# A gated recurrent layer on one core: GpSimd's addition for an output goes behind its work on 1-z, and VectorE's addition of two x sums goes to the middle of a half step

## The chip, the core and the metric

The kernel runs on one core of one Trainium2 chip. The engines in this text are TensorE (PE, with its weight loads PEld), VectorE (DVE), ScalarE (ACT), GpSimd (POOL) and the queue that issues transfers (SP). The metric is device time in microseconds (us). Before the change it is 1883.74 us, the median of three runs (1882.47 to 1884.24).

## The reference

All arrays are float32. x is 64 x 128 x 512 (batch, time, feature). Two layers follow one another, and each adds its input to its result. Layer 0 is a gated scan that isn't touched here. Layer 1 is a recurrence over 128 time steps with a state h of 64 x 512:

```
xz, xr, xh = seq @ W_z, seq @ W_r, seq @ W
def step(h, xs):
    z  = sigmoid(xzt + h @ U_z + vz)
    r  = sigmoid(xrt + h @ U_r + vr)
    hh = tanh(xht + r * h @ U + vh)
    h_new = (1.0 - z) * h + z * hh
    return (h_new, h_new)
x = x + layer1(x)
```

So each output row is the new h plus that time step's x. vz, vr and vh come from a conditioning vector and are the same for all time steps.

## The kernel before, in words

**Two streams.** The 64 batches are cut into two streams of 32 (`SB`), and their time steps alternate: while one stream waits for its gates, TensorE works for the other. One time step of one stream is called a half step in this text, and the function `halves` (a generator) writes it down in two parts. All instructions are pinned, so each engine runs its instructions in the order in which the program names them; nothing is reordered later.

**One half step.** Part one: TensorE multiplies the old state hT with the weights of r and z (the groups `g<-w_s,h`, L464); ScalarE takes the sigmoid of r (L918); VectorE forms r*h and transposes it, in two halves (L922, L923, L922, L923); ScalarE takes the sigmoid of z (L927); GpSimd forms 1-z (L933) and (1-z)*h (L934). Part two: TensorE multiplies the transposed r*h with the candidate's weights (the groups `g<-w_s,fi`, L464, "the candidate group" below); ScalarE takes the tanh (L957); VectorE forms the new h (L969, L970) and transposes it to hT (L974). Then GpSimd adds x to hT (L985, into the tile hh), and in the next half step, which is the other stream's, VectorE transposes that sum into the output tile (L994, the function `output`, kept in the list `deferred` until then).

**The x products.** The products of x with W_z, W_r and W don't depend on the state. They are computed ahead of the recurrence, for windows of eight time steps, with a fast matrix multiplication in two nested levels (seven products for eight, twice). Its products are TensorE groups at L602 (`r`, `r12a`, `r12b`, `shared`), and `place` puts up to three of them into each half step, to fill TensorE while the gates are worked out. What the scheme costs elsewhere: GpSimd makes sums and differences of x (L810, `take_sums`, into `held`); VectorE reads the products out of PSUM, with an addition to an accumulator in SBUF (L704) or with an addition of a common part (L699), both in `read`; VectorE adds two accumulators, both in SBUF, in `add_c` (L719); GpSimd does the same for another pair in `add` (L724). The finished sums are stored to DRAM (`shares`) and loaded again as a stream's start value for its gates (`load_share`, L865; `put_share`, L871).

**The order around the change.** The mid of a half step, between the two parts, is written like this:

```
add(1)
take_sums(2 if busy else 3)
place(targets()[0], busy)
...
read(reads[0] and max(reads[0], len(to_read) - 2))
while deferred:
    deferred.pop(0)()
```

At the end of part two stand L985, `deferred.append(output)`, then `add_c()` and `read(reads[1])`. `reads` is (4, 1) in the first stretch and (4, 0) later, so mostly up to four reads stand in the mid. `add_c` takes one entry from the list `to_add_c`, if there is one; the reading of the sixth of the seven outer products (`n == 5`) calls it by itself for a block that still waits (`while n == 5 and (m, j) in waiting_c`). `waiting`, `to_add` and `add` are the same for GpSimd. From time step 121 on (`APART`) another form of the half step runs, without L985.

Of the kernel before, what the change touches and what calls it, by code (L numbers as in the profile page):

```python
# [12 lines left out]
ALU = mybir.AluOpType  # L13
# [6 lines left out]
def kernel(  # L20
# [38 lines left out]
    nc = tc.nc  # L59
# [11 lines left out]
    SB = B // 2  # L71
# [7 lines left out]
    def pin(instruction):  # L79
        return tc.keep_in_program_order(instruction)  # L80
# [199 lines left out]
    def chunk_products(g, c, between=None):  # L280

        f, i = fs[c % 2], is_[c % 2]
        fb, ib = by_batch(f), by_batch(i)
        p = gate(g, c, 0)
        pin(nc.scalar.activation(fb, p, AF.Sigmoid, bias=biasT[:, 0, c : c + 1]))
        if g == 0 and c == 0:
            w0_transposed(0, 2)
        elif g == 0 and c + 1 < K:
            w0_transposed(c + 1, 0)
        if between:  # L290
            between()
        p = gate(g, c, 1)
        pin(nc.scalar.activation(ib, p, AF.Sigmoid, bias=biasT[:, 0, K + c : K + c + 1]))
        if g == 0 and c == 0:
            transposed(condT, cond_sb, n=B)
            w0_transposed(1, 0)
        elif g == 0 and c + 1 < K:
            w0_transposed(c + 1, 1)
        if g + 1 < NG:
            for u, m in ((), ((0, 0), (0, 1)), ((1, 0),), ((1, 1),))[c]:  # L300
                x_joined(g + 1, u, m)
        p = gate(g, c, 2)
        if g == 0 and c + 1 < K:
            for n in range(1 if c == 0 else 2, 3):
                w0_transposed(c + 1, n)
        return p
# [135 lines left out]
    def conditioning():  # L442

        vs = []
        for s in range(2):
            p = psum.tile([P, 3, P], F32, tag="tp", name=f"pv{s}")
            matmuls(p, lambda k: condT[:, k, s * SB : (s + 1) * SB], [cw[:, k] for k in range(K)])
            whole = const.tile([P, 3, P], F32, name=f"whole_v{s}")
            pin(nc.vector.tensor_tensor(whole, p, bias1, ALU.add))
            vs.append(whole)  # L450
        return vs
# [106 lines left out]
    def x_of(st, t):  # L558

        return x4[t // TH][:, :, t % TH, st.batches]  # L560
# [4 lines left out]
    class Outer:  # L565
# [121 lines left out]
        def read(self, block, common):  # L687


            (m, j), n, r = block, self.n, self.bank(block)  # L690

            while n in (0, 5) and (m, j) in waiting:
                add(1)
            while n == 5 and (m, j) in waiting_c:
                add_c()
            if j == 1 and not common:
                if not hasattr(self, "common"):
                    shared_to_copy[0]()
                pin(nc.vector.tensor_tensor(r, r, self.common, ALU.add))  # L699
                return  # L700
            u, s5, c = (acc[:, i, m, j] for i in range(3))
            v1, v21 = v_x[:, j], v_x[:, 2 + j]
            dst, other = ((u, v1), (c, u), (u, u), (s5, v21), (c, s5), (u, u), (c, u))[n]
            pin(nc.vector.tensor_tensor(dst, r, other, ALU.add))  # L704
            unread.discard(r.name)
            if n == 1:
                self.store(c, 0, m, j)
            elif n == 4:
                waiting_c.add((m, j))
                to_add_c.append(lambda: self.add_c(c, u, m, j))  # L710
            elif n == 5:
                waiting.add((m, j))
                to_add.append(lambda: self.add(s5, u, m, j))
            elif n == 6:
                self.store(c, 1, m, j)

        def add_c(self, c, u, m, j):
            waiting_c.remove((m, j))
            pin(nc.vector.tensor_tensor(c, c, u, ALU.add))  # L719
            self.store(c, 0, m, 2 + j)  # L720

        def add(self, s5, u, m, j):
            waiting.remove((m, j))
            pin(nc.gpsimd.tensor_tensor(s5, s5, u, ALU.add))  # L724
            self.store(s5, 1, m, 2 + j)
# [13 lines left out]
    to_copy, shared_to_copy = [], []  # L739
    to_read, unread = [], set()  # L740
# [12 lines left out]
    sums_to_take, taken = [], set()  # L753
# [12 lines left out]
    def sum_tasks(group):  # L766
# [24 lines left out]
        def halves(d):  # L791
            *ts, op = d
            return [(*[t[:, k] for t in ts], op) for k in range(HC)]

        outer = [
            [(base - 1, ("s", group, i, k), d_) for k, d_ in enumerate(halves(d))]
            for i, d in enumerate(wsums(x_[0][0], x_[0][1], x_[1][0], x_[1][1], s_))
        ]
# [6 lines left out]
    def take_sums(n):  # L805
        for m in range(n):
            if not sums_to_take or sums_to_take[0][0] > state["begun"]:
                return m
            _, name, a = sums_to_take.pop(0)
            pin(nc.gpsimd.tensor_tensor(*a))  # L810
            taken.add(name)
        return n

    ahead = []
# [21 lines left out]
    class Stream:  # L836
# [56 lines left out]
        def halves(self, t, filler=None, between=None, targets=lambda: (0, 0), busy=False, reads=(4, 0)):  # L893
# [40 lines left out]
                    pin(nc.gpsimd.tensor_tensor(r, r, h_, ALU.mult))  # L934
            while shared_to_copy:
                shared_to_copy[0]()
            add(1)
            take_sums(2 if busy else 3)
            place(targets()[0], busy)
            if filler:  # L940
                filler()
            read(reads[0] and max(reads[0], len(to_read) - 2))
            while deferred:
                deferred.pop(0)()
# [4 lines left out]
            h, hT, hh = (tile_[:, n] for n in range(3))  # L949
# [31 lines left out]
            if apart:  # L981
                deferred.append(output)
                return
            pin(
                nc.gpsimd.tensor_tensor(  # L985
                    hh.rearrange("p (k b) -> p k b", b=SB),
                    hT.rearrange("p (k b) -> p k b", b=SB),
                    x_of(self, t),
                    ALU.add,
                )  # L990
            )

            def output():
                pin(nc.vector.transpose(o, hh))  # L994
                self.store(t)

            deferred.append(output)
            if APART <= t + AHEAD < S:

                pin(nc.gpsimd.tensor_copy(ident.rearrange("p (k b) -> p k b", b=SB), x_of(self, t + AHEAD)))  # L1000
                deferred.append(lambda: pin(nc.vector.transpose(self.output(t + AHEAD), ident)))
            add_c()
            read(reads[1])
            if t + 2 < S and not direct(self, t + 2) and all((t + 2, q) in stored for q in range(Q)):
                self.load_share(t + 2)
# [29 lines left out]
    APART, AHEAD = 121, 10  # L1035
    last_outputs = []
    deferred = []
    pending = []

    shares_d = [dram.tile([TW * B, Q, 3 * P], F32, name=f"shares{n}") for n in range(4)]  # L1040

    for g in range(NG):
        for c in range(K):
# [7 lines left out]
            if (g, c) == (1, 1):  # L1051
                vs = []
                p = chunk_products(g, c, between=lambda: vs.extend(conditioning()))
            else:
                p = chunk_products(g, c)
# [154 lines left out]
    for n in range(2):  # L1210
        t = work.tile([P, 5, 3, P], F32, tag="xt", bufs=2, name=f"w_inner{n}")
# [94 lines left out]
        n += len(steps)  # L1306
    while deferred:
        deferred.pop(0)()
    assert not ahead and not to_read and not to_copy and not shared_to_copy and not sums_to_take


# [32 lines left out]
```

## Time and profile before

| | |
|---|---|
| median of the three runs | 1883.74 us |
| the profiled execution, its own time | 1881.64 us |
| its span, from the first to the last instruction | 1879.9 us |
| TensorE busy | 1864.0 us, 99% of the span |
| VectorE busy | 1504.4 us, 80% |
| GpSimd busy | 864.1 us, 46% |
| granted TensorE clock | 1.00 |
| layer 1 in the trace | from about 684 us to the end |
| VectorE's additions L719 | 60, mean 556 ns |
| GpSimd's additions L985 | 242, mean 501 ns |

The profile is of one execution. "Busy" is the time in which an engine has an instruction; the number behind an `x` counts instructions (a float32 matmul leaves two records). A timeline row gives the start in us from the span's start, the duration in us, engine, line, operation, the tiles written and read, and, in brackets, the idle time before it and what ended it. Releasers are inferred. Engines that aren't the bottleneck may idle at no cost.

### The profile page before, as it was taken

The numbers are of one execution on the slowest core, as the hardware profiler recorded it, in microseconds if no ns is written. First come the engines' busy times: TensorE is split into PE (matmuls) and PEld (weight loads), VectorE is DVE, ScalarE is ACT, GpSimd is POOL, SyncE is SP. The second block draws the span as 40 slices with busy tenths as digits, with TensorE's granted clock in tenths as the row PEclk, the third lists the DMA queues.
The fourth block names the chain that finished last, engine by engine and source line by source line (L and its number), as shares of the span: only waits on it lengthen the run. The fifth ranks groups of instructions, "written<-read, shape, count | busy, mean of one in ns | idle before, by whom it ended". The sixth has DMA issues, their size and how long they took to land.

```text
span 1879.9 us, 62310 instructions
## 1 busy us (share of the span) xinstructions
PE 1864.0 (99%) x24793; PEld 1061.1 (56%) x24793; DVE 1504.4 (80%) x3438; ACT 722.3 (38%) x1888; POOL 864.1 (46%) x1544
## 2 busy tenths in 40 slices
PE   9999999999999999999999999999999999999998
PEld 5444444444444445666666666666666666666667
DVE  5899999999999977577777777777777777777786
ACT  3232223222232232344444444444444444444444
POOL 1233232333323244446556566566565565565650
PEclk9999999999999999999999999999999999999999
DMA  7765433433343240334334344344343343443343
GB/s 176 182 124 117 84 69 74 88 81 80 73 80 60 49 86 29 96 94 141 104 105 131 108 116 130 100 129 121 101 140 108 99 139 103 115 130 96 111 110 79
DMA packets 366754, 195.38 MB, mean 104 GB/s; under 512 B 225332, under 2 KB 352064, under 8 KB 366464
## 3 DMA queue, kind: packets, MB, share of 16 engines
q1 hardware_dynamic: 366280, 191.33, 41.0%
q8 instruction: 195, 3.19, 0.7%
q14 instruction: 95, 0.78, 0.2%
q10 hardware_dynamic: 184, 0.07, 0.0%
HBM read 78.63 MB, written 81.13 MB: 85 GB/s over the span
## 4 chain that ended last, share of the span: by engine, by line
PE 97%; DVE 1%; issue 0%; DMA 0%; ACT 0%; SPq 0%; DVEq 0%; ACTq 0%
PE g L464 36%; PE p L232 35%; PE r L602 14%; PE r12a L602 4%; PE shared L602 4%; PE r12b L602 4%; PE gz L464 1%; PE tp L190 0%; PE pv L464 0%; DMA x<-in_x_dram 0%; DVE W L704 0%; DMA out_dram<-o_last 0%; DVE fi L923 0%; DVE fi L922 0%; DVE r L339 0%
## 5 line engine op out<-in xcount | busy, mean ns | idle before, releaser
L232 PE MATMUL p<-xT,W 128*128 128x512 f32 (+1 forms) x1560 | 661.9, 586 | 0.1
L232 PEld LDWEIGHTS p<-xT,W 128*128 128x128 f32 x1560 | 293.4, 190 | 361.6 <-issue 359.4
L464 PE MATMUL g<-w_s,h 128*32 128x256 f32 (+1 forms) x8128 | 481.3, 373 | 2.6 <-issue 1.4
L464 PEld LDWEIGHTS g<-w_s,h 128*32 128x32 f32 x8128 | 304.1, 110 | 177.0 <-issue 81.8
L464 PEld LDWEIGHTS g<-w_s,fi 128*32 128x32 f32 x8128 | 222.9, 109 | 116.1 <-issue 57.9
L464 PE MATMUL g<-w_s,fi 128*32 128x128 f32 x8128 | 276.0, 273 | 5.4 <-DVE fi L922 3.9
L922 DVE TENSOR_TENSOR fi<-fi,h 128x64 f32<-128x64 f32 (+1 forms) x494 | 112.5, 228 | 172.3 <-ACT fi L918 171.2
L985 POOL TENSOR_TENSOR h<-h,x 128x128 f32<-128x128 f32 x242 | 121.3, 501 | 234.1 <-DVE h L974 207.8
L314 POOL COPY first<-condT 128x4 f32<-128x4 f32 x64 | 12.4, 194 | 461.7 <-DVE h L386 431.9
L918 ACT ACTIVATE fi<-g 128x128 f32<-128x128 f32 x254 | 70.6, 278 | 324.2 <-PE g L464 305.1
L933 POOL TENSOR_SCALAR fi<-fi 128x128 f32<-128x128 f32 x240 | 71.9, 300 | 239.4 <-DVE fi L922 231.1
L704 DVE TENSOR_TENSOR W<-r,W 128x384 f32<-128x384 f32 x315 | 169.3, 539 | 7.5
L310 ACT ACTIVATE fi<-fi 128x512 f32<-128x512 f32 x64 | 40.3, 630 | 340.4 <-DVE fi L351 340.4
L957 ACT ACTIVATE h<-g 128x128 f32<-128x128 f32 x256 | 71.2, 278 | 241.8 <-PE g L464 241.8
L923 DVE STREAM_TRANSPOSE fi<-fi 128x64 f32<-128x64 f32 (+1 forms) x494 | 122.2, 247 | 22.8 <-PE r12a L602 0.5
L969 DVE TENSOR_TENSOR h<-h,fi 128x128 f32<-128x128 f32 (+1 forms) x264 | 93.8, 355 | 53.9 <-ACT h L957 53.1
L253 POOL TENSOR_TENSOR x<-xT,h 128x512 f32<-128x512 f32 x63 | 122.6, 1946 | 4.9
L934 POOL TENSOR_TENSOR fi<-fi,h 128x128 f32<-128x128 f32 x240 | 110.2, 459 | 20.0
L970 DVE TENSOR_TENSOR h<-h,fi 128x128 f32<-128x128 f32 (+1 forms) x264 | 97.6, 370 | 27.2 <-POOL held L810 0.9
L602 PE MATMUL r<-w_inner,held 128*32 128x384 f32 x1080 | 114.8, 486 | 0.0
L810 POOL TENSOR_TENSOR held<-held 128x128 f32<-128x128 f32 x240 | 112.9, 485 | 3.1
L339 DVE RECIPROCAL r<-r 128x256 f32<-128x256 f32 x60 | 104.4, 1740 | 0.0
(153 smaller groups left out, 2727.7 us busy)
## 6 DMA issues: line engine op xcount, KB each, us to landing
shares<-W SPq DMA_DIRECT2D x240, 192.0 KB, 2.0
xz<-shares SPq DMA_DIRECT2D x480, 48.0 KB, 1.9
whole_v<-shares SPq DMA_DIRECT2D x480, 48.0 KB, 1.9
x2d<-x SPq DMA_DIRECT2D x63, 256.0 KB, 4.5
words<-held SPq DMA_DIRECT2D x240, 64.0 KB, 2.1
out_dram<-o SPq DMA_DIRECT2D x240, 64.0 KB, 1.8
xw_None<-x2d SPq DMA_DIRECT2D x56, 256.0 KB, 3.3
w_rows<-in_L_cond_W_f_dram SPq DMA_DIRECT2D x4, 256.0 KB, 5.8
```

Source lines behind the costliest of these rows:

```text
L232: nc.tensor.matmul(p[:, tokens], lhsT=W0[:, c, n, k, :], rhs=xT[g][:, k, tokens], start=(k == 0), stop=(k == K - 1),)
L253: nc.gpsimd.tensor_tensor(x2.rearrange("p (t b) -> p t b", b=GB)[:, ts], xT[g][:, c, :].rearrange(f"{layout(g)} -> p t b", b=GB)[:, ts], b ...
L339: pin(nc.vector.reciprocal(r, r))
L464: nc.tensor.matmul(p[q * SB : (q + 1) * SB], lhsT=lhsT(k), rhs=part(wk, q), start=(start and k == 0), stop=(stop and k == len(w) - 1), ski ...
L602: nc.tensor.matmul(self.bank(bank)[q * SB : (q + 1) * SB], lhsT=a[:, q * SB : (q + 1) * SB], rhs=w_, start=start, stop=True, skip_group_ch ...
L704: pin(nc.vector.tensor_tensor(dst, r, other, ALU.add))
L810: pin(nc.gpsimd.tensor_tensor(*a))
L922: pin(nc.vector.tensor_tensor(rh[:, e], r[:, e], h_[:, e], ALU.mult))
L923: pin(nc.vector.transpose(rhT[:, e], rh[:, e]))
L934: pin(nc.gpsimd.tensor_tensor(r, r, h_, ALU.mult))
L970: pin(nc.vector.tensor_tensor(h[:, e], hh[:, e], r[:, e], ALU.add))
L985: nc.gpsimd.tensor_tensor(hh.rearrange("p (k b) -> p k b", b=SB), hT.rearrange("p (k b) -> p k b", b=SB), x_of(self, t), ALU.add,)
```

## The change

Two things move in `halves`; no instruction is added or taken out.

- L985 is put off. Instead of writing it down at the end of its half step, the code keeps it in a new list `unsummed` and writes it down in the next half step, behind L933 and L934 and ahead of `add(1)` and `take_sums`. It appends `output` to `deferred` only then, and `deferred` is still worked off in that same half step.
- `add_c()` goes from the end of part two to the mid of the half step, ahead of `read`, and runs there only if fewer than four reads are due.

```
             while shared_to_copy:
                 shared_to_copy[0]()
+            while unsummed:
+                unsummed.pop(0)()
             add(1)
             take_sums(2 if busy else 3)
             place(targets()[0], busy)
             if filler:
                 filler()
+            if len(to_read) < 4:
+                add_c()
             read(reads[0] and max(reads[0], len(to_read) - 2))
...
-            pin(
-                nc.gpsimd.tensor_tensor(
-                    hh.rearrange("p (k b) -> p k b", b=SB),
-                    hT.rearrange("p (k b) -> p k b", b=SB),
-                    x_of(self, t),
-                    ALU.add,
-                )
-            )
...
-            deferred.append(output)
+            def summed():
+                pin(
+                    nc.gpsimd.tensor_tensor(
+                        hh.rearrange("p (k b) -> p k b", b=SB),
+                        hT.rearrange("p (k b) -> p k b", b=SB),
+                        x_of(self, t),
+                        ALU.add,
+                    )
+                )
+                deferred.append(output)
+
+            unsummed.append(summed)
...
-            add_c()
             read(reads[1])
...
+    unsummed = []
```

More of the change, by code (lines that the diff above doesn't have):

```diff
@@ L1308 @@
         deferred.pop(0)()
-    assert not ahead and not to_read and not to_copy and not shared_to_copy and not sums_to_take
+    assert not ahead and not to_read and not to_copy and not shared_to_copy and not sums_to_take and not unsummed
 _INS = [
```

## The prediction

> **What bounds the kernel now.** I read the page's busy times first, then its chain of work that ended last.
>
> ```profile
> PE 1864.0 (99%) x24793; PEld 1061.1 (56%) x24793; DVE 1504.4 (80%) x3438; ACT 722.3 (38%) x1888; POOL 864.1 (46%) x1544
> ...
> PE 97%; DVE 1%; issue 0%; DMA 0%; ACT 0%; SPq 0%; DVEq 0%; ACTq 0%
> ```
>
> TensorE is the bound, and the change takes no work from it. So it can only shorten or lengthen waits of TensorE, and these must be found although TensorE counts as busy. In the timeline, the candidate groups (`g<-w_s,fi`) start at 1292.99 and 1297.52: an undisturbed half step takes 4.53 us (5.18 where it holds one more x product of 0.65). I took the distances of all these starts between 720 and 1797 us; what exceeds 4.53 or 5.18 is a stall. The sum is only about 7.5 us, in pieces of 0.02 to 0.5. Next I looked at what lies ahead of such a stall, on all engines.
>
> ```profile
> 1064.73 0.52 DVE L719 TENSOR_TENSOR W<-W 128x384 f32<-128x384 f32 x1
> ...
> 1064.95 0.62 POOL L985 TENSOR_TENSOR h<-h,x 128x128 f32<-128x128 f32 x1 [2.31 <-DVE h L974]
> ...
> 1065.17 0.48 DVE L922 TENSOR_TENSOR fi<-fi,h 128x64 f32<-128x64 f32 x1
> ...
> 1065.68 0.24 DVE L923 STREAM_TRANSPOSE fi<-fi 128x64 f32<-128x64 f32 x1
> ...
> 1066.08 1.08 PE L464 MATMUL g<-w_s,fi 128*32 128x128 f32 x32
> ```
>
> L922 takes 0.23 us undisturbed (0.18 behind another instruction) and 0.48 here. It ends at 1065.65, 0.08 after L985 (1065.57); L985 itself took 0.62 instead of 0.46, as it began during L719. So an addition of VectorE with two inputs in SBUF (L719, L922, L969, L970) and one of GpSimd exclude each other. The transposes and the readers of PSUM (L704, L699) keep their durations beside GpSimd. The transposed r*h releases the candidate group, and that group began 0.21 late. Both halves of the change touch this place.
>
> **Part one: L985 moves behind L933 and L934.** Its 242 executions stay. In half steps with few GpSimd sums L985 now runs alone between L974 and L922; later it runs from about 0.9 to 1.35 us after the candidate group's start, when VectorE reads PSUM. I counted 23 half steps from 853 to 1797 us whose L922 is stretched by L985 and whose sums (L810) are long over; their stalls add up to 2.4 us. Some of these have three sums, which now end 0.4 later and delay L970: 0.2 off. Gain 2.2. Between 1797 and 1836 four such stalls (0.40, 0.20, 0.06, 0.04) give 0.5.
>
> Where L724 and three sums follow, nothing is won: GpSimd runs without a pause to about 3.4 to 4.0 us after the group's start, L985 last. Put first, it pushes L724 and L810 back by its spacing of 0.42, so that the last L810 meets L922 instead. I replayed three kinds of such half steps by the rows of their own instructions (1302.09, 936.60, 867.43): L922 ends within 0.04 of where it did. I take 0; bounds -1.0 and +2.0 over some 40 half steps.
>
> One early stall is large: the candidate group at 714.40 is 2.75 late. There L985 holds back four sums of 128x256 until 709.43, where they alternate with L1278 and three L515, which take about 1.0 each instead of 0.55. After the change these sums no longer wait for L974 and can start about 1.6 earlier, beside PSUM reads. I take 1.0; bounds 0.3 and 1.8.
>
> What waits for L985: L994, next half step. The slack between them was 0.67 to several us; L985 now ends about 1.4 after the group's start, so L994 waits only with one or two reads ahead of it, and delays L969 by up to 0.25. That is covered by VectorE's idle time ahead of L922 (171.2 us in 210 waits). Behind L985 on GpSimd stand L724 and the sums; TensorE starts a product 2.57 us or more after its sum in 95 of 100 cases.
>
> **Part two: L719.** In the order of the built program 46 of the 60 stand behind L974 before and none after. The condition on the reads due holds them back in half steps with four reads, and they pile up. In the listing a half step never had more than one L719 (after 800 us); now eight have three and four have two, always ahead of or between three or four reads. This is such a half step before:
>
> ```profile
> 1292.92 0.24 DVE L923 STREAM_TRANSPOSE fi<-fi 128x64 f32<-128x64 f32 x1
> 1293.26 0.56 DVE L704 TENSOR_TENSOR W<-r,W 128x384 f32<-128x384 f32 x1
> 1293.73 0.56 DVE L699 TENSOR_TENSOR r<-r,x 128x384 f32<-128x384 f32 x1
> 1294.32 0.56 DVE L704 TENSOR_TENSOR W<-r,W 128x384 f32<-128x384 f32 x1
> 1294.79 0.55 DVE L719 TENSOR_TENSOR W<-W 128x384 f32<-128x384 f32 x1
> 1295.26 0.56 DVE L699 TENSOR_TENSOR r12a<-r12a,x 128x384 f32<-128x384 f32 x1
> ...
> 1296.63 0.31 DVE L974 STREAM_TRANSPOSE h<-h 128x128 f32<-128x128 f32 x1
> 1296.87 0.18 DVE L922 TENSOR_TENSOR fi<-fi,h 128x64 f32<-128x64 f32 x1
> ```
>
> VectorE has no idle time left: L922 comes right behind L974, and the next candidate group still starts on time, with 0.05 to spare. The half step gets two more L719, one ahead of the first L704 and one between it and L699. By the spacing of starts (0.44 to 0.48 for each, and 0.16 won since the first need not wait for PSUM) L922 comes 0.74 later. That is TensorE's wait without any exclusion: **0.7**. With it more: rows where L719 meets GpSimd follow.
>
> ```profile
> 779.81 0.72 POOL L933 TENSOR_SCALAR fi<-fi 128x128 f32<-128x128 f32 x1 [5.26 <-DVE fi L922]
> 779.85 0.52 DVE L719 TENSOR_TENSOR W<-W 128x384 f32<-128x384 f32 x1
> ...
> 1589.37 0.46 POOL L934 TENSOR_TENSOR fi<-fi,h 128x128 f32<-128x128 f32 x1
> 1589.47 0.77 DVE L719 TENSOR_TENSOR W<-W 128x384 f32<-128x384 f32 x1
> 1589.78 1.33 POOL L724 TENSOR_TENSOR W<-W 128x384 f32<-128x384 f32 x1
> ```
>
> The first L719 comes right behind L923, as in the first two rows, and delays L933, L934 and L985; the second then meets L934 or L985, the third L724 (+0.2 to +0.4 each by these rows). L922 comes 1.02 later (1.14 if L933 goes first).
>
> - Five half steps of this kind (three L719, four reads), at 1219, 1293, 1367, 1441 and 1515: 4 x 1.0, and 0.3 for the one at 1441, which has an x product more. 4.3 (without exclusion 2.9, at most 4.9).
> - Three at 923, 997 and 1071 (three L719, three reads, one L719 before): 0.9 each less the 0.1 stalled now. 2.4 (0.9 to 2.5).
> - At 1145 a product of TensorE waits for a read (L704 ends 1146.40, L602 starts 1146.45); one L719 is now ahead: 0.4.
> - Three at 1589, 1662 and 1736 (two L719 for one): 0.35 each, 1.05 (0.7 to 1.8).
>
> Sum **8.2**, bounds 4.9 and 9.6. TensorE can't make a wait good: no other work of its order is ready. Transfers: one more start value is loaded at the head of a half step (12 for 11 before); no ScalarE copy L871 waits for a load in the waits view. Cost 0.
>
> The Trainium skill (SBUF — State Buffer, "Who interferes with whom") says that a VectorE instruction with two SBUF inputs and a GpSimd one that reads SBUF exclude each other for the whole instruction, whoever starts first. By that rule a blocked L719 would add its whole 0.52 after the other's end; the row at 1589.47 shows 0.41 (1590.24 less 1589.83). With 0.52 two blocked L719 in each of eleven of these half steps would make the sum 2 us larger. The row decides.
>
> **Sum.** 8.2 - 2.2 - 0.5 - 1.0 = +4.5 us. The profiled execution goes from 1881.64 to 1886.1. Its time is 2.1 below the median, so for the median I say 1883.74 + 4.5 = **1888.2**.
>
> **Rivals.**
> 1. *The additions meet GpSimd less than counted* (order of starts falls well, early gain 1.8). Losses 4.9, gains up to 5.5: -0.6 to +2.5, about 1885. For it: an L719 that starts first isn't slowed. Against: GpSimd is busy at these places without a pause.
> 2. *The late sums now block L922.* In half steps with L724 and three sums L922 waits for an L810 of up to 0.78 instead of an L985 of 0.46: 0.2 more in some 25 half steps, +5, with the sum above +9.5, about 1893. Against: my replays; for: the last L810 is often the longer instruction.
> 3. *Faster: all exclusions vanish.* If the gaps that L985 leaves let the sums end before L922 everywhere, the 7.5 us of stalls, 0.7 at the end and 1.8 early all go: -10.0, and with losses of 4.9 the time is 1878.6. It decides from the point where the twelve crowded half steps cost less than what is won. Against: GpSimd's amount of work is the same, and in 40 half steps it has no gap.
>
> **How the numbers follow.** Forecast (+2.5 to +7) 0.52, rival 1 0.27, rival 2 0.16, rival 3 0.05. The range joins the bounds: losses 4.9 less gains 5.5 gives 1883; losses 9.6, gains 2.2 and +2.0 in the half steps with many sums give 1893. A measurement of this kernel can tell about 0.2% (3.8 us) from no change: slower by more is 0.4 of the forecast's 0.52 and all of rival 2, 0.56; faster by more 0.04; within 0.40.
>
> **What would show it.** In the profile after: L922's stretched executions in half steps without late sums are gone; the half steps named above take 5.2 to 5.6 us from one candidate group to the next, with L974 and L922 late behind three L719; the stall at 714 shrinks. I am wrong if those half steps keep 4.53, or if L922 waits for L810 in many others.

## The result, and the profile after

The changed kernel takes 1889.68 us (median of 6 runs, 1889.42 to 1890.39); the kernel before, on the same chip, 1882.97 (6 runs, 1881.90 to 1884.24). The ratio is 1.0036, with a 95% interval from 1.0026 to 1.0047: 6.7 us slower. The profiled executions have spans of 1888.1 and 1879.9 us, 8.2 apart, at granted clocks of 1.00; the before profile was of one of its quicker executions.

In the code behind the change L985 is L996, and its transpose L994 is L991; L957, L969, L970, L974 are L961, L973, L974, L978. The lines up to L934 keep their numbers. The page after, its busy line and the shares of the chain of work that ended last:

```profile
PE 1865.7 (99%) x24793; PEld 1071.1 (57%) x24793; DVE 1526.7 (81%) x3438; ACT 722.8 (38%) x1888; POOL 858.0 (45%) x1544
...
PE 88%; DVE 6%; POOL 2%; issue 1%; ACT 1%; DMA 0%; SPq 0%; DVEq 0%; POOLq 0%; ACTq 0%
```

TensorE has the same instructions and is busy 1.7 us longer; the rest of the 8.2 are pauses. The chain now runs over VectorE and GpSimd for 8% of the span (before, 1%). The groups of instructions by line, busy time and mean, then idle time before them and its cause:

```profile
L464 PE MATMUL g<-w_s,fi 128*32 128x128 f32 x8128 | 276.1, 273 | 10.6 <-DVE fi L922 9.8
...
L922 DVE TENSOR_TENSOR fi<-fi,h 128x64 f32<-128x64 f32 (+1 forms) x494 | 106.9, 216 | 161.0 <-ACT fi L918 159.8
...
L991 DVE STREAM_TRANSPOSE o<-h 128x128 f32<-128x128 f32 x240 | 73.1, 305 | 52.4 <-POOL h L996 48.1
...
L996 POOL TENSOR_TENSOR h<-h,x 128x128 f32<-128x128 f32 x242 | 113.7, 470 | 3.1 <-DVE h L978 3.1
```

L922 and L996 got shorter (means 228 and 501 ns before): they meet less, as part one should bring. L991 waits 48.1 us for L996, where its wait for GpSimd was 0.6. Most of that stands in place of idle time that was there: VectorE's waits ahead of L922 (for L918) and of L973 (for L961) went from 171.2 and 53.1 to 159.8 and 17.8 us. The candidate group waits 9.8 us for L922, and here the time went. This is the crowded half step whose before-form the prediction shows at 1293, one window later (timeline of after):

```profile
1370.46 0.25 DVE L923 STREAM_TRANSPOSE fi<-fi 128x64 f32<-128x64 f32 x1
...
1370.48 1.08 PE L464 MATMUL g<-w_s,fi 128*32 128x128 f32 x32
1370.59 0.72 POOL L933 TENSOR_SCALAR fi<-fi 128x128 f32<-128x128 f32 x1 [1.47 <-DVE fi L922]
1370.63 0.52 DVE L719 TENSOR_TENSOR W<-W 128x384 f32<-128x384 f32 x1
...
1371.25 0.56 DVE L704 TENSOR_TENSOR W<-r,W 128x384 f32<-128x384 f32 x1
...
1371.72 0.55 DVE L719 TENSOR_TENSOR W<-W 128x384 f32<-128x384 f32 x1
1371.81 0.78 POOL L996 TENSOR_TENSOR h<-h,x 128x128 f32<-128x128 f32 x1
...
1372.19 0.56 DVE L699 TENSOR_TENSOR r<-r,x 128x384 f32<-128x384 f32 x1
...
1372.56 1.00 POOL L724 TENSOR_TENSOR W<-W 128x384 f32<-128x384 f32 x1
1372.78 0.56 DVE L704 TENSOR_TENSOR W<-r,W 128x384 f32<-128x384 f32 x1
1373.26 0.71 DVE L719 TENSOR_TENSOR W<-W 128x384 f32<-128x384 f32 x1
...
1375.43 0.18 DVE L922 TENSOR_TENSOR fi<-fi,h 128x64 f32<-128x64 f32 x1
```

VectorE works without a pause from L923 to L922. L922 starts 4.95 us after the candidate group's start, where it started 3.88 after it in the form before (1296.87 less 1292.99): 1.07 later. The next candidate group is 1.03 late (5.56 instead of 4.53).

**Where the 8.2 us of the spans are.** I added up what the distances between candidate groups have over 4.53 or 5.18, as in the prediction, for both profiles. The last row holds whole times.

| stretch | before | after | predicted change | measured |
|---|---|---|---|---|
| 684 to 720 us (the early stall among them) | 4.00 | 2.74 | -1.0 | -1.3 |
| the twelve crowded half steps | 0.8 | 9.4 | +8.2 | +8.6 |
| 22 half steps with L724 and several sums | 3.4 | 5.2 | 0 | +1.8 |
| all other half steps of 860 to 1797 | 4.4 | 3.2 | -2.2 | -1.2 |
| the end: from the candidate group at 1796.16 (after: 1803.92) to the end of the span | 83.7 | 84.2 | -0.5 | +0.5 |

The sum of the measured column is +8.4. Layer 1's first candidate group is 0.1 earlier (688.31, before 688.44); the rest of the difference to 8.2 is rounding.

### The profile page after: what moved, and what is told of

Its sections match the earlier page's. It is cut to its first block, busy times and chain, and to the rows that moved or that the text cites. A ratio compares the mean times of both kernels' runs of the same rounds, so it can differ in the third digit from the quotient of the medians.

```text
span 1888.1 us, 61983 instructions
## 1 busy us (share of the span) xinstructions
PE 1865.7 (99%) x24793; PEld 1071.1 (57%) x24793; DVE 1526.7 (81%) x3438; ACT 722.8 (38%) x1888; POOL 858.0 (45%) x1544
## 4 chain that ended last, share of the span: by engine, by line
PE 88%; DVE 6%; POOL 2%; issue 1%; ACT 1%; DMA 0%; SPq 0%; DVEq 0%; POOLq 0%; ACTq 0%
PE p L232 35%; PE g L464 32%; PE r L602 12%; PE shared L602 3%; PE r12a L602 3%; PE r12b L602 3%; POOL held L810 1%; DVE fi L922 1%; DVE W L704 1%; DVE fi L923 1%; DVE W L719 1%; ACT fi L918 1%; POOL fi L933 1%; PE gz L464 0%; DVE h L974 0%
## 5 line engine op out<-in xcount | busy, mean ns | idle before, releaser
L464 PEld LDWEIGHTS g<-w_s,h 128*32 128x32 f32 x8128 | 313.3, 110 | 167.8 <-issue 79.3
L933 POOL TENSOR_SCALAR fi<-fi 128x128 f32<-128x128 f32 x240 | 86.6, 361 | 481.5 <-DVE fi L922 417.0
L922 DVE TENSOR_TENSOR fi<-fi,h 128x64 f32<-128x64 f32 (+1 forms) x494 | 106.9, 216 | 161.0 <-ACT fi L918 159.8
L918 ACT ACTIVATE fi<-g 128x128 f32<-128x128 f32 x254 | 70.5, 278 | 332.2 <-PE g L464 229.0
L704 DVE TENSOR_TENSOR W<-r,W 128x384 f32<-128x384 f32 x315 | 169.7, 540 | 6.9
L961 ACT ACTIVATE h<-g 128x128 f32<-128x128 f32 x256 | 71.2, 278 | 244.5 <-PE g L464 244.5
L923 DVE STREAM_TRANSPOSE fi<-fi 128x64 f32<-128x64 f32 (+1 forms) x494 | 122.3, 248 | 22.5
L934 POOL TENSOR_TENSOR fi<-fi,h 128x128 f32<-128x128 f32 x240 | 111.4, 464 | 20.0
L974 DVE TENSOR_TENSOR h<-h,fi 128x128 f32<-128x128 f32 (+1 forms) x264 | 112.9, 428 | 9.1
L973 DVE TENSOR_TENSOR h<-h,fi 128x128 f32<-128x128 f32 (+1 forms) x264 | 102.5, 388 | 18.1 <-ACT h L961 17.8
L991 DVE STREAM_TRANSPOSE o<-h 128x128 f32<-128x128 f32 x240 | 73.1, 305 | 52.4 <-POOL h L996 48.1
L996 POOL TENSOR_TENSOR h<-h,x 128x128 f32<-128x128 f32 x242 | 113.7, 470 | 3.1 <-DVE h L978 3.1
L810 POOL TENSOR_TENSOR held<-held 128x128 f32<-128x128 f32 x240 | 110.4, 475 | 3.1
```

Source lines behind the costliest of these rows:

```text
L464: nc.tensor.matmul(p[q * SB : (q + 1) * SB], lhsT=lhsT(k), rhs=part(wk, q), start=(start and k == 0), stop=(stop and k == len(w) - 1), ski ...
L922: pin(nc.vector.tensor_tensor(rh[:, e], r[:, e], h_[:, e], ALU.mult))
L923: pin(nc.vector.transpose(rhT[:, e], rh[:, e]))
L933: pin(nc.gpsimd.tensor_scalar(r, z, -1.0, 1.0, ALU.mult, ALU.add))
L974: pin(nc.vector.tensor_tensor(h[:, e], hh[:, e], r[:, e], ALU.add))
L996: nc.gpsimd.tensor_tensor(hh.rearrange("p (k b) -> p k b", b=SB), hT.rearrange("p (k b) -> p k b", b=SB), x_of(self, t), ALU.add,)
```

## Experiments

All times are medians, with the kernel before run on the same chip. Where stalls are named, they are read from each run's own profile as in the table.

**Part one alone.** L985 moves, L719 stays:

```diff
-            if len(to_read) < 4:
-                add_c()
             read(reads[0] and max(reads[0], len(to_read) - 2))
...
             unsummed.append(summed)
...
+            add_c()
             read(reads[1])
```

> Only L985 moves; L719 stays behind the transpose of the new h. Theory A (the time is lost in half steps into which several L719 are crowded): none of these half steps is crowded any more, so the 8.6 us that they lose in the changed kernel are absent, and what is left is the balance of L985: about 1.3 us won at the early stall, 2.2 in half steps with few sums, 1.7 to 3 lost in half steps with many sums. Total -2 to +1 us against the kernel before. Rival B (L985 pushes the sums of GpSimd onto VectorE's r*h, and this is the loss): +5 to +8 us.

Measured: 1881.5 us (11 runs) against 1882.56; ratio 0.9997 (0.9988 to 1.0006). Part one by itself changes next to nothing that a measurement can tell. Its profile has the early gain (2.74 as after) and the stalls of 0.21 to 0.32 in the half steps with L724 and several sums (5.3 us in 22 of them; before, 3.4), and no crowded half step. But four of the half steps that are crowded in the changed kernel (near 1219, 1293, 1367 and 1515) lose 0.26 to 0.29 here too, with one L719 each: L985 ahead of L724 pushes L724 back, from 0.85 us after the candidate group (1293.84 less 1292.99, before) to 1.33, and the L719 that is there meets it and takes 0.95 instead of 0.55 (timeline; the group starts at 1291.59):

```profile
1292.92 1.01 POOL L724 TENSOR_TENSOR W<-W 128x384 f32<-128x384 f32 x1
...
1293.40 0.95 DVE L719 TENSOR_TENSOR W<-W 128x384 f32<-128x384 f32 x1
```

**Part two alone.** L719 moves, L985 stays at the end of its half step:

```diff
+            if len(to_read) < 4:
+                add_c()
             read(reads[0] and max(reads[0], len(to_read) - 2))
...
-            add_c()
             read(reads[1])
```

> Only L719 moves; L985 stays at the end of its half step. Theory A: the twelve crowded half steps lose 8 to 9 us, of which the L719 that no longer stand ahead of r*h give back about 1: +6 to +9 us against the kernel before. Rival B: 0 to +2 us. Theory A in the timeline: a half step with three L719 and four reads takes 5.4 to 5.6 us from one candidate group to the next.

Measured: 1892.1 us (5 runs) against 1882.56; ratio 1.0049 (1.0035 to 1.0063). The crowded half steps lose 1.06, 1.07, 1.06, 0.41 and 1.06 (three L719, four reads), 0.65 three times, 1.17 at 1147, and 0.41 to 0.43 three times. So the pile-up of L719 costs the time, with or without part one. One stall of about 1.7 at 715 to 718 in this profile is none of part two's: the granted TensorE clock was 0.54 there, and 1.00 before and after it (windows; us, busy times by engine, then the granted clock, the DMA share and GB/s):

```profile
714.80:718.50 3.70, 3.70 (x37) 1.70 (x32) 3.56 (x8) 1.22 (x3) 3.29 (x6) 0.54 0.29 64
```

3.70 us at 0.46 less clock make the 1.7. It comes right behind the early stall, in which TensorE waits for 2.57 us. The kernel before has the same wait, and no such stretch in its profile. How many of the other four runs had it isn't known.

**At most one in each half step.** Both parts, but without the condition on the reads due:

```diff
-            if len(to_read) < 4:
-                add_c()
+            add_c()
             read(reads[0] and max(reads[0], len(to_read) - 2))
```

> Both parts, but one L719 is taken in the mid of every half step, however many reads are due. By the order of the program no half step then holds three L719 (after 800 us); eleven hold two, eight of these with four reads. Theory A, with the number of L719 in a half step as the cause: the ones with two L719 and four reads lose 0.4 each (as measured for such half steps in the changed kernel), the ones that lost 0.85 lose 0.1 or nothing; +1 to +4 us against the kernel before. Rival C (the place in the mid is bad by itself, wherever GpSimd works on 1-z): +6 to +9 us as in the changed kernel.

Measured: 1886.3 us (11 runs) against 1882.56; ratio 1.0020 (1.0011 to 1.0029), 3 us better than the changed kernel. No half step has three L719 after 800 us. Of the eight with two L719 and four reads, three lose 0.39, as expected, one 0.06, and four 0.68 to 0.71: there the second L719 comes on top of L724 and takes 1.05. These four are the ones that lose 0.26 to 0.29 with part one alone, so the L719 that is added costs about 0.4 in them too. The condition is thus what piles them up, but to write L719 ahead of four reads costs without it too.

**The crowd without L985 and L724.** The changed kernel with L996 and L724 taken out, so that VectorE meets hardly any addition of GpSimd in the crowded half steps. The output lacks x, and a quarter of the x sums lacks a term:

```diff
-            pin(nc.gpsimd.tensor_tensor(s5, s5, u, ALU.add))
...
-                pin(nc.vector.transpose(o, hh))
+                pin(nc.vector.transpose(o, hT))
...
             def summed():
-                pin(nc.gpsimd.tensor_tensor(... hT ..., x_of(self, t), ALU.add))
                 deferred.append(output)
```

> The changed kernel without two GpSimd additions: L985 (the output then lacks x) and L724 (one quarter of the x sums is then wrong). The crowded half steps stay, with less GpSimd work beside them. If VectorE's own work is what they lack time for, a half step with three L719 and four reads still loses 0.8 to 0.9 us (1.02 in the changed kernel); if the exclusion with L985 and L724 makes a large part, as the prediction had it (0.3 of 1.0), it loses 0.7 or less. The total falls below the kernel before by up to 2 us or stays within 2 us above it, since all stalls from L985 and L724 go.

Measured: 1879.38 us (one run), span 1877.6. The crowded half steps with four reads still lose 0.88 to 0.89 (1.02 in the changed kernel), those with three reads 0.65 (0.85), those with two L719 0.41 to 0.42 (0.40). VectorE's part of such a half step (timeline; the lines stand one lower here, so L923 is L922 and L922 is L921):

```profile
1290.86 0.25 DVE L922 STREAM_TRANSPOSE fi<-fi 128x64 f32<-128x64 f32 x1
1291.03 0.52 DVE L719 TENSOR_TENSOR W<-W 128x384 f32<-128x384 f32 x1
1291.65 0.56 DVE L704 TENSOR_TENSOR W<-r,W 128x384 f32<-128x384 f32 x1
1292.12 0.55 DVE L719 TENSOR_TENSOR W<-W 128x384 f32<-128x384 f32 x1
1292.59 0.56 DVE L699 TENSOR_TENSOR r<-r,x 128x384 f32<-128x384 f32 x1
1293.18 0.56 DVE L704 TENSOR_TENSOR W<-r,W 128x384 f32<-128x384 f32 x1
1293.66 0.55 DVE L719 TENSOR_TENSOR W<-W 128x384 f32<-128x384 f32 x1
```

The third L719 takes 0.55 instead of 0.71: without L724 no L719 is stretched. But L704 comes 0.62 after the first L719's start, where two neighbours are usually 0.44 to 0.48 apart. In the built program this L704 adds to the accumulator that L719 has just written, and it has a wait for VectorE's own result; so has the L704 behind L699, which reads the sum that L699 wrote and comes 0.59 after it. In the kernel with at most one L719 in each half step, where the first L704 behind L719 has no such wait, it comes 0.44 after it (1294.13 less 1293.69). So L704 waits for that result, 0.16.

**No L985 at all.** The kernel before without L985; its transpose takes hT, so the output lacks x:

```diff
-            pin(nc.gpsimd.tensor_tensor(... hT ..., x_of(self, t), ALU.add))
...
-                pin(nc.vector.transpose(o, hh))
+                pin(nc.vector.transpose(o, hT))
```

> The kernel before without L985: VectorE transposes the new h itself into the output, so the output lacks x in the non-final part. It bounds what any place for L985 can win. By the stalls of the kernel before: 2.4 in half steps with few sums, about 1.2 at the early stall, 0.5 near the end, and up to 2 of the 3.4 in half steps with many sums: -4 to -6.5 us. If the place of L985 hardly matters (rival), -2 to 0.

Measured: 1875.55 us (5 runs) against 1882.66; ratio 0.9963 (0.9950 to 0.9975). I take it as the bound of what a place of L985 can give: about 7 us. Its profile still has 2.1 us in the 22 half steps with many sums, and its end is as long as before (83.6 us; before, 83.7), where 0.5 less was expected.

**L985 behind the sums.** L719 stays; L985 is written in the next half step, behind `add(1)` and `take_sums`, and its transpose one half step later still (against part one alone):

```diff
-            while unsummed:
-                unsummed.pop(0)()
             add(1)
             take_sums(2 if busy else 3)
             place(targets()[0], busy)
+            ready = deferred[:]
+            deferred.clear()
+            while unsummed:
+                unsummed.pop(0)()
...
-            while deferred:
-                deferred.pop(0)()
+            while ready:
+                ready.pop(0)()
```

> L985 moves to the next half step as in the change, but behind the sums there, and the transpose that reads it comes one half step later; L719 stays where it was. Theory: the half steps with few sums win as with part one (2.2), the ones with many sums lose nothing, since L724 and the sums start as early as before, and r's sigmoid (L918) waits for two engines as before and starts 0.06 us after its matmuls instead of 0.11: -2.5 to -4.5 us. If part one's lost gain had another cause than the pushed sums and the additional wait: -1 to +0.5, as with part one alone.

Measured: 1878.83 us (11 runs) against 1882.66; ratio 0.9979 (0.9970 to 0.9988), 4 us faster. The time is as expected, the way to it only in part. The gain is 1.6 us up to 797 and 2.7 in the half steps with few sums, and no 0.07 is lost to the sigmoid of r. But the 22 half steps with many sums, which were to lose nothing more, lose 5.2 instead of 3.4: L985 (L996 here) now stands behind the sums and meets L922 itself (timeline):

```profile
943.17 0.45 POOL L996 TENSOR_TENSOR h<-h,x 128x128 f32<-128x128 f32 x1
943.20 0.50 DVE L922 TENSOR_TENSOR fi<-fi,h 128x64 f32<-128x64 f32 x1 [0.65 <-ACT fi L918]
```

**L985 between L933 and L934.** Part one, but one instruction earlier:

```diff
                     pin(nc.gpsimd.tensor_scalar(r, z, -1.0, 1.0, ALU.mult, ALU.add))
+                    while unsummed:
+                        unsummed.pop(0)()
                     pin(nc.gpsimd.tensor_tensor(r, r, h_, ALU.mult))
```

> As part one alone, but L985 stands between L933 and L934. Then L970 again waits for L934 itself, as before the change, and r's sigmoid (L918) needs no wait for GpSimd of its own. Theory D (this wait makes the sigmoid 0.05 late in some 155 half steps, which shows as stalls of 0.07 in the 20 or so that have no slack): these stalls go, L918 starts 0.06 after its matmuls; about 1.2 us less than part one alone, -1 to -3 us against the kernel before. The half steps with many sums still lose 0.23 to 0.30, as with part one. If the 0.07 stalls come from the sums beside VectorE: no change against part one alone (-1.5 to +1).

Measured: 1876.92 us (6 runs) against 1882.66; ratio 0.9968 (0.9956 to 0.9979). It is 5.7 us faster than the kernel before, some 13 faster than the changed one: more than I had expected. One instruction's place makes 4.6 us between this kernel and part one alone. Two things changed, and the profiles show both. First GpSimd in the same half step, part one alone and then this kernel (timelines; L994 and L996 are L985, L936 is L934):

```profile
940.01 0.30 POOL L933 TENSOR_SCALAR fi<-fi 128x128 f32<-128x128 f32 x1 [0.63 <-ACT r L615]
940.39 0.46 POOL L934 TENSOR_TENSOR fi<-fi,h 128x128 f32<-128x128 f32 x1
940.81 0.46 POOL L994 TENSOR_TENSOR h<-h,x 128x128 f32<-128x128 f32 x1
941.23 1.01 POOL L724 TENSOR_TENSOR W<-W 128x384 f32<-128x384 f32 x1
```

```profile
939.59 0.30 POOL L933 TENSOR_SCALAR fi<-fi 128x128 f32<-128x128 f32 x1 [0.63 <-DVE fi L922]
939.85 0.46 POOL L996 TENSOR_TENSOR h<-h,x 128x128 f32<-128x128 f32 x1
940.27 0.46 POOL L936 TENSOR_TENSOR fi<-fi,h 128x128 f32<-128x128 f32 x1
940.68 1.02 POOL L724 TENSOR_TENSOR W<-W 128x384 f32<-128x384 f32 x1
```

L934 needs L933's result and starts 0.38 after it. With L985 in that gap the next instruction starts after 0.26, and L724 comes 1.09 after L933 instead of 1.22. All sums end that much earlier, and the last one meets L922 for less: the 22 half steps lose 2.2 us instead of 5.3. Second, the waits view of ScalarE for its sigmoid of r (total us, times, longest), for before, after, and this kernel:

```profile
ACT fi L918 <- POOL held L810: 5.0, 4, 1.3
```

```profile
ACT fi L918 <- POOL held L810: 57.3, 50, 1.9
```

```profile
ACT fi L918 <- PE g L464: 315.6, 246, 3.3
```

In the changed kernel, and in part one alone, the built program gives L918 a third wait, on GpSimd (for L934; the view names the last thing that GpSimd did). Before, VectorE's L970 had that wait, and L918 was covered by it. With L985 behind L934 and VectorE's transpose waiting for L985, L970 needs no wait of its own, and so L918 gets one. The semaphores in the traces show this: L970 waits for GpSimd 240 times before and in this kernel, and never in the changed one; L918 does so in 51 of 254 cases before and in 223 after, and in 177 of these it has waits for VectorE, TensorE and GpSimd (the expectation's 155 were too few). The wait for the matmuls then stands in an instruction of its own ahead of L918, and L918 starts 0.04 to 0.05 after that one has ended (in 176 of the 177). L934 is long done, yet L918 starts 0.05 later behind its matmuls: 0.11 or more in 221 of the 223 cases, 0.06 or so in 201 of the 202 that waited for TensorE last before the change. In the crowded half step above, which started at 1370.48, it starts 3.56 after the candidate group; in its form before, at 1292.99, it was 3.51 (timelines, after and before):

```profile
1374.04 0.28 ACT L918 ACTIVATE fi<-g 128x128 f32<-128x128 f32 x1 [1.25 <-POOL W L724]
```

```profile
1296.50 0.28 ACT L918 ACTIVATE fi<-g 128x128 f32<-128x128 f32 x1 [1.20 <-PE g L464]
```

Where the spare was 0.05, that is a stall of 0.06 or 0.07: 24 of these in part one alone, 1.5 us in sum; none here and none with L985 behind the sums. By the profiles the two come to 3.1 and 1.5 us, together the 4.6.

**Fewer sums at a time.** L985 behind the sums, and only one sum instead of three where an L724 is due:

```diff
+            both = to_add[:1]
             add(1)
-            take_sums(2 if busy else 3)
+            take_sums(2 if busy else 1 if both else 3)
```

> As L985 behind the sums, and where L724 is due only one sum is taken instead of three, the others one or more half steps later. If the crowded GpSimd half steps (L724 and three sums) are what is left of the steady stalls, their 0.2 to 0.3 go: another 1.5 to 2.5 us below that kernel, -4 to -6.5 us against the kernel before. If the late sums make TensorE wait instead: 0 to +4.

Measured: 2052.18 us (4 runs) against 1882.66; ratio 1.0907 (1.0890 to 1.0924). A clear miss. The waits view of TensorE:

```profile
PE shared L602 <- POOL held L810: 53.9, 21, 3.9
PE r L602 <- POOL held L810: 36.4, 21, 2.8
PE r12a L602 <- POOL held L810: 24.1, 13, 2.5
PE r12b L602 <- POOL held L810: 20.6, 11, 2.5
```

The x products now wait 135 us for their sums, put off too far. The busy time of TensorE grew by 41.6 us as well (1901.9 against 1860.3 with L985 in between). The table by windows shows one reason (us, busy times by engine, then the granted clock in front of the DMA share):

```profile
200.00:600.00 400.00, 400.00 (x934) 177.10 (x933) 370.87 (x399) 116.30 (x163) 132.47 (x117) 1.00 0.39 78
800.00:1000.00 200.00, 171.61 (x3115) 102.34 (x3104) 121.06 (x386) 73.58 (x221) 86.68 (x189) 0.96 0.36 97
```

With TensorE idle for 14% of a stretch the granted clock is 0.96 there. That mean is made of 18 stretches in which the granted clock was 0.5: sixteen of 3.41 us and two of 6.83, of which TensorE was busy 64.0 in sum. At half the clock 32.0 of this is lost time, of the 41.6; the rest stays open. 135 and 41.6 together are, within about 1 us, the 175.5 between these two spans.

**Both parts, L985 in between.** The changed kernel, with L985 one instruction earlier. Do the two costs add up?

```diff
                     pin(nc.gpsimd.tensor_scalar(r, z, -1.0, 1.0, ALU.mult, ALU.add))
+                    while unsummed:
+                        unsummed.pop(0)()
                     pin(nc.gpsimd.tensor_tensor(r, r, h_, ALU.mult))
```

> The changed kernel, with L985 between L933 and L934 instead of behind both. It asks whether the two parts' costs add up. Theory A (they do: the place of L985 costs about 4.6 us, the difference between part one alone and part one with L985 in between, 1881.5 and 1876.9, and the pile-up of L719 costs the rest whatever L985 does): about 1889.7 - 4.6 = 1885.1 us; the five half steps with three L719 and four reads still lose 0.95 to 1.05 each, the half steps with many sums 0.05 to 0.2, and the 0.07 stalls in undisturbed half steps go. Theory B (where L719 comes right behind L923 it delays L933 and all behind it, so the place of L985 gives nothing once L719 has moved): 1888 us or more.

Measured: 1887.82 us (6 runs) against 1882.95; ratio 1.0031 (1.0019 to 1.0043). Neither theory: 1.9 better than the changed kernel, not 4.6. The crowded half steps lose more, 1.33 to 1.35 (four of the five with four reads) and 0.70 to 0.71 (the fifth, and those with two L719). The timeline of one of them:

```profile
1295.02 0.46 POOL L936 TENSOR_TENSOR fi<-fi,h 128x128 f32<-128x128 f32 x1
...
1295.06 0.84 DVE L719 TENSOR_TENSOR W<-W 128x384 f32<-128x384 f32 x1
...
1295.44 1.33 POOL L724 TENSOR_TENSOR W<-W 128x384 f32<-128x384 f32 x1
```

The second L719 now comes 0.04 behind the start of L934 and is held back until it ends (0.84 instead of 0.55). In the changed kernel it started 0.09 ahead of L985, and GpSimd's instruction was the one stretched (0.78). So 0.1 us in the order of two starts decides which of the engines pays; eight half steps times 0.31 is 2.5 of the 2.7 us that are missing.

**L719 behind the reads.** The changed kernel, same condition:

```diff
-            if len(to_read) < 4:
-                add_c()
+            few = len(to_read) < 4
             read(reads[0] and max(reads[0], len(to_read) - 2))
+            if few:
+                add_c()
```

> The changed kernel, with the same condition on L719 but with its place behind the reads of the half step instead of ahead of them (the n == 5 calls are as they were). As many L719 pile up in the same half steps. Theory A (VectorE's own amount of work makes 0.74 of the 1.02 lost in each crowded half step, and the place ahead of the reads the rest: L704 waits for L719's result, 0.16, and L719 runs against L933 and L934): the crowded half steps with four reads lose 0.75 to 0.9, those with two L719 0.25 to 0.4, in all 1 to 2.5 us less than the changed kernel, about 1888. Theory B (the place doesn't matter, or L719 meets the sums instead): the crowded half steps keep 1.0 or more and the time is 1889.5 or longer.

Measured: 1884.41 us (11 runs) against 1882.95; ratio 1.0009 (1.0001 to 1.0018). It is 5.3 better than the changed kernel, far more than expected, since one premise was wrong: a read queues an L719 that the same half step can now take, so the crowded half steps hold two instead of three. Four of the five with four reads lose 0.58 to 0.60, the fifth nothing, and those with three reads 0.25. The loss of the four fits the count: one L719 more than before, 0.55 to the next start here, and 0.17 more for the one stretched by L724, less small pieces; 0.26 to 0.29 of it is lost with part one alone already. What the place alone does, at the same number of L719, isn't settled by this run.

## Why the prediction was right, and where it was not

The mechanism was as predicted: L719 piles up in half steps in which VectorE has no idle time, and each such half step delays L922 and TensorE. Point by point:

- **Crowded half steps, +8.2 predicted, +8.6 measured.** Three L719 and four reads: 1.03, 1.03, 1.03, 0.39 and 1.04 (1.0 and 0.3 predicted). The ones near 923, 997, 1071: 0.84 to 0.86 (0.9). The one at 1145: 0.7 more (0.4). Two L719 for one: 0.40 each (0.35). The size is right, but its making was not. I gave 0.74 to VectorE's own work and 0.28 to exclusion. Without L985 and L724 0.88 of it remains: 0.16 is L704 waiting for L719's result, a wait that I hadn't counted; 0.14 is what L985 and L724 add. That the two errors cancel, and 1.02 came out, is luck. Of the three L719 only the third is stretched. The second isn't delayed by L985, as the prediction had it: it delays L985.
- **Early stall, -1.0 predicted, -1.3 measured.** The sums no longer wait for L985 there. GpSimd's timeline after, with the four sums of 128x256 that took 2.47 and 2.03 before, from 709.43:

```profile
707.21 1.48 POOL L810 TENSOR_TENSOR held<-x 128x256 f32<-128x256 f32 x2
708.65 1.48 POOL L810 TENSOR_TENSOR held<-held,x 128x256 f32<-128x256 f32 x2
```

- **Light half steps, -2.2 predicted, -1.2 measured.** The stretched L922 are gone (2.1 us in eleven half steps of 0.12 to 0.23, and smaller ones), and with some other stalls 3.1 us are won. What the prediction lacked is the sigmoid's third wait, which gives back about 1.1, and three new stalls of 0.22 to 0.35, 0.8 in sum, whose cause I haven't followed.
- **Half steps with L724 and several sums, 0 predicted, +1.8 measured**, inside the bound of +2.0. Of the three kinds that I replayed, two came out (936.60 and 1302.09 still lose 0.21 to 0.24), one did not: the kind of 867.43 loses 0.22 to 0.30 instead of 0.08. The timeline of one, GpSimd's and VectorE's rows as two answers of the same kernel:

```profile
942.22 1.00 POOL L724 TENSOR_TENSOR W<-W 128x384 f32<-128x384 f32 x1
943.18 1.52 POOL L810 TENSOR_TENSOR held<-held,x 128x256 f32<-128x256 f32 x2
944.66 0.46 POOL L810 TENSOR_TENSOR held<-x 128x128 f32<-128x128 f32 x1
```

```profile
943.40 0.70 DVE L974 TENSOR_TENSOR h<-h,fi 128x128 f32<-128x128 f32 x1
944.14 0.31 DVE L978 STREAM_TRANSPOSE h<-h 128x128 f32<-128x128 f32 x1
944.74 0.46 DVE L922 TENSOR_TENSOR fi<-fi,h 128x64 f32<-128x64 f32 x1 [0.29 <-ACT fi L918]
```

The last L810 starts 0.08 ahead of L922, which takes 0.46 instead of 0.23. This is the second rival's mechanism, in one kind of half step, of which there are nine.
- **The end, -0.5 predicted, +0.5 measured: failed.** A half step takes only 3.89 there. Of four half steps from 1808 on three had an L719 before, behind the transpose of the new h; all four have one after, ahead of the reads. They lose 0.25, 0.08, 0.39 and 0.25, where they lost 0.41, 0.01, 0.21 and 0.01: L922 is no longer stretched by 0.25 (once by 0.13), but starts later. I had counted the L985 that goes and not the L719 that comes. That is 0.3 of the 0.5; the rest is spread over small pieces that I could not place.
- **The sum.** +4.5 predicted, +6.7 between the medians and +8.2 between the two spans. The terms that were missed are, in us, 1.8 (many sums), 1.0 (the end) and 1.0 (light half steps).

The third rival, faster by all exclusions gone, has no support: without L985 the kernel gains 7 us, and part one alone has about 1 of them. That place, more than the idea of a later half step, is what kept part one from gaining: one instruction earlier, between L933 and L934, it gives 5.7.

The Trainium skill (SBUF — State Buffer, "Who interferes with whom") has the engine that issues first keep the shared ports for the whole instruction. Here the order of starts does decide who is stretched, but not always: L933 starts 0.04 ahead of L719 (1370.59 and 1370.63) and takes 0.72 instead of 0.30, while L719 keeps 0.52.

## What to carry to other kernels

Before an instruction is moved to a place with a condition, list in the built program how many of them each stage will hold: an average that fits says nothing of stages in which three come together and the engine has no idle time. The engine next door counts by the order of starts to a tenth of a microsecond, so try an off-path instruction in several neighbouring places, a gap that a dependency leaves on its own engine first. Look also for waits that change hands: a wait that one engine no longer needs can turn up on another that has no spare.

## What was not expected of the hardware

- One more wait, on a semaphore that had long been reached, came with a start of ScalarE's sigmoid 0.05 us later (0.11 behind the last matmul instead of 0.06), in 177 half steps of the changed kernel.
- Two neighbouring VectorE additions are 0.44 to 0.48 us apart, but 0.59 or 0.62 when the second reads what the first has just written.
- The granted TensorE clock was 0.96 in stretches of 200 us in which TensorE waited for 11 to 14% of the time, and 1.00 where it didn't wait. Within them it is either 1.00 or 0.5: in the kernel with fewer sums at a time and in part two alone it falls to 0.5 nineteen times before the last matmul, at times that lie on a grid of 3.41 us in each trace, and each time TensorE was busy for at most 1.37 us of the 3.41 before. After none of the stretches of that grid with 1.46 us or more did it fall. So the place of one wait of 2.57 us on this grid can make 1.7 us, as in part two alone.
